# Local attention on 64x64 quarters of the matmul array: all of its products, and the last rows of the gated products

## The chip, the core and the metric

The kernel runs on one core of one Trainium2 chip. The metric is device time in microseconds (us): 3955.65 us is the median of three runs before the change (3954.25 to 3959.32). The core has a matmul engine (PE in the profile, with its weight loads as PEld), VectorE (DVE), ScalarE (ACT), GpSimd (POOL), and DMA queues, of which SyncE's (SP) carries nearly all of the traffic here. Matmuls write to PSUM, eight banks of 128 partitions x 512 fp32 values; VectorE and ScalarE carry the results on to SBUF.

## The reference, cut to what matters

A block of eight sequences of 512 tokens and 256 channels goes through three residual steps: a small transformer (two layers, added with the factor 0.5), a global attention, and the small transformer once more. All is fp32. One layer of the small transformer, as far as it matters here:

```python
def _layer(x, wqkv, qs, ksc, wo, lg, lb, w1, b1, w2, b2):
    h = shift_token(x)                        # second half of the channels from the token before
    q, k, v = jnp.split(h @ wqkv, 3, axis=-1) # 8 heads of 64
    q, k = rotary_xpos(l2norm(q) * qs, l2norm(k) * ksc)
    x = x + local_attention(q, k, v) @ wo
    h = layernorm(shift_token(x)) * lg + lb
    a, g = jnp.split(h @ w1 + b1, 2, axis=-1) # 682 and 682 channels
    return x + (a * gelu(g)) @ w2 + b2
```

In `local_attention` a window has 128 tokens; queries of a window see their own window and the one before:

```python
    sim = jnp.einsum('bhwid,bhwjd->bhwij', bq, bk)
    mask = (i < j) | (i > j + WINDOW) | (j == -1)
    attn = jax.nn.softmax(jnp.where(mask, -big, sim), axis=-1)
    out = jnp.einsum('bhwij,bhwjd->bhwid', attn, bv)
```

So query i of a window sees the keys 0 to i of its own window and the keys i to 127 of the window before. In halves of 64: the second half of the own keys is seen by the second half of the queries only, and the first half of the keys of the window before by the first half of the queries only.

## The kernel before

A sequence is 4 tiles of 128 tokens, and a window is one tile. Two streams, `stream(0, ...)` and `stream(1, ...)`, each take four sequences through the small transformer twice, eight blocks a stream, and a third stream (`global_stream`) computes the global attention, head by head, of sequences whose first transformer is done. The three are Python generators that only record operations.

The order in which operations are issued is not written down. `Plan.record` collects each operation with its inputs and outputs, and `Plan.order` schedules them greedily: at each step it takes, on the engine that can start earliest, the operation of lowest rank that is ready within 40 ns. It uses the costs of `Plan.cost`, keeps a pool of slots for every buffer (the eight PSUM banks among them), and for the matmul engine it counts a change of array shape: an operation's shape is its `op.mode`, a change is priced by `MODE`, and `STICK` lets operations of the present shape go first. Operations recorded within `plan.together()` stay together. `Plan.issue` then issues every operation from one line, L369, so the profile tells groups apart by the names of their tiles.

The array can be used whole (128 rows x 128 columns of weights), in two halves by rows (64x128: `halves`), by columns (128x64: `columns`), in four quarters (64x64: `quarters`), or in strips of 32 rows (`fours`, used for the scores of the global attention). Products on different parts run side by side.

`attention(k, y, l, far)` handles one sequence and layer. `front(t)` makes q, k and v of tile t; `scores(t, ...)` the probabilities; `values(t, ...)` the products with v; `project(t, o)` the output projection. `far` is true for blocks 1 to 6 of a stream (24 attentions) and false for the first and the last block (8 attentions, called "near" in this text). The two forms differ in how they turn tiles: far turns q, k and the probabilities with VectorE's 32x32 transposes and a round trip through DRAM; near uses transposes on the matmul engine, which go to a PSUM bank and are copied by ScalarE (`work_both` in the profile).

Before the change:

- Scores of far tiles 1 to 3 (`quarters` in the code) run in four 64x64 quarters and leave out the masked half windows (192 of 256 columns). Scores of near tiles and of far tile 0 run in two halves, one head of a pair in each, with 128 query columns of weights and 128 or 256 key columns moving. The two heads of a pair go to two banks.
- Values of far tiles 1 to 3 run in quarters, the two halves of the keys into two PSUM banks, `pos[0]` and `pos[1]`. ScalarE copies the first to `o`, and VectorE adds the second. Values of near tiles and of far tile 0 run by columns, all 128 keys of a window at once, one bank `po`, which ScalarE copies to `o`.
- In `glu`, the hidden width is 682 = 5 x 128 + 42. The last 42 rows and one row for the bias (43 in all) of two token tiles lie at partitions 0 and 64; their products run in two halves, one per tile, at the end of each pair of tiles.

Of the kernel before, what the change touches and what calls it, by code (L numbers as in the profile page):

```python
# [15 lines left out]
P = 128  # L16
B, N, D = 8, 512, 256
NT = N // P
DEPTH, HEADS, DH, WINDOW = 2, 8, 64, 128
INNER = HEADS * DH  # L20
NPAIR = HEADS // 2
HID = int(D * 4 * 2 / 3)
NHC = -(-HID // P)
FULL = NHC - 1
LAST = HID - FULL * P
HALF = P // 2
# [150 lines left out]
class Plan:  # L177
# [55 lines left out]
    def cost(self, op):  # L233

        if op.engine == "tensor":

            lanes, op.mode = {}, "whole"
            for name, args, kw in op.calls:
                lane, t = 0, 109.0
                if name == "matmul":  # L240
                    a = kw["lhsT"]
                    lane, t = (a.region()[0], args[0].region()[0]), 2 * max(0.842 * elements(kw["rhs"]), 0.852 * a.shape[1])
                    k, m = a.shape
                    op.mode = "fours" if k <= 32 else "quarters" if k == m == 64 else "halves" if k <= 64 else "columns" if m <= 64 else "whole"
                lanes[lane] = lanes.get(lane, 0.0) + t
            busy = max(lanes.values())
            return busy, busy + 170
        name, args, kw = op.calls[0]
        n = max(elements(a) for a in (*args, *kw.values()) if hasattr(a, "shape"))
        if name == "dma_start":  # L250
            return 580.0, 2300.0
        if op.engine == "scalar":
            if name == "activation":
                op.mode = {AF.Exp: "exp", AF.Gelu: "gelu"}.get(args[2])
                busy = 70 + 0.82 * n + (105 if "bias" in kw else 0)
                return (busy + 93, busy + 310) if "accum_out" in kw else (busy, busy + 110)
            return 70 + 0.81 * n, 175 + 0.81 * n
        if op.engine == "vector":
            if name == "tensor_tensor_reduce":
                return 90.0 + n, 250.0 + n  # L260
            if name == "bn_stats":
                return 70.0 + n, 150.0 + n
            return 90 + 1.035 * n, 170 + 1.035 * n
        if name == "memset":
            return 80 + 0.85 * n, 100 + 0.85 * n
        if ALU.pow in args:
            return 350.0 + 157 * n, 400.0 + 157 * n
        return 210 + 1.98 * n, 250 + 1.98 * n
# [107 lines left out]
def macaron(ctx: ExitStack, tc: tile.TileContext, x, weight, wqkv, wo, w1, w2, b2, vecs, qk_scales, rotary, out):  # L376
    nc = plan = Plan()
# [121 lines left out]
    def bank(shape):  # L499
        return psum.tile(shape, F32, tag="bank", width=N)  # L500
# [65 lines left out]
    def attention(k, y, l, far):  # L566
# [5 lines left out]
        v = {}  # L572
# [57 lines left out]
        def scores(t, pair, rn):  # L630
# [14 lines left out]
            nk = min(t, 1) + 1  # L645
            kinds = slice((t + 1) % 2, (t + 1) % 2 + nk)
            mk = mask[:, kinds, :].rearrange("p j k -> p (j k)")
            probs = []
# [3 lines left out]
            for g in range(2):  # L652

                quarters = far and nk == 2
                sps = [bank([P, 2, 3 * HALF if quarters else nk * P]) for _ in range(2)]

                pieces = [(slice(0, P), slice(0, nk * P), slice(0, nk * P))]
                if quarters:

                    pieces = []  # L660
                    for half in range(2):
                        q = slice(half * HALF, (half + 1) * HALF)
# [6 lines left out]
                with plan.together():  # L669
                    for i in range(2):  # L670
                        keys = kT[:, 2 * g + i].rearrange("p j k -> p (j k)")
                        for q, to, ks in sorted(pieces, key=lambda piece: piece[1].start - piece[1].stop):
                            for par in range(2):
                                rows = slice(par * DH, (par + 1) * DH)
# [17 lines left out]
                for par in range(2):  # L692
                    for i in range(2):
                        h = 2 * i + par
# [11 lines left out]
                for par in range(2):  # L706
                    for i in range(2):
                        h = 2 * i + par
# [23 lines left out]
        def values(t, probs):  # L732

            nk = min(t, 1) + 1
            o = work.tile([P, NPAIR, P], F32, tag="o", bufs=2)
            if far and nk == 2:

                pos = [bank([P, NPAIR, P]) for _ in range(2)]
                for g in range(2):
                    with plan.together():  # L740
                        for i in range(2):
                            for n in range(2):
                                for half in range(2):

                                    j = (1 - half, half)[n]
                                    q = slice(half * 2, half * 2 + 2) if n else slice(0, 4)
                                    rows = slice(half * HALF, (half + 1) * HALF)
                                    for par in range(2):
                                        h = 2 * i + par
                                        hd = 4 * g + h  # L750
                                        nc.tensor.matmul(
                                            pos[half][par * DH : (par + 1) * DH, 2 * g + i, q.start * 32 : q.stop * 32],
                                            lhsT=v[t - 1 + j][rows, hd * DH : (hd + 1) * DH],
                                            rhs=probs[g][rows, j, q, h, :],
                                            start=(n == 0),
                                            stop=(n == 1),
                                        )
                nc.scalar.copy(o, pos[0])
                nc.vector.tensor_add(o, pos[1], o)
                return o  # L760
            po = bank([P, NPAIR, P])

            def products(pair, turned):
                for j in range(nk):
                    for par in range(2):
                        hd = 2 * pair + par
                        nc.tensor.matmul(
                            po[par * DH : (par + 1) * DH, pair, :],
                            lhsT=v[t - (t + j) % 2][:, hd * DH : (hd + 1) * DH],
                            rhs=turned(par, j),  # L770
                            start=(j == 0),
                            stop=(j == nk - 1),
                        )

            if far:
                for g in range(2):
                    with plan.together():
                        for i in range(2):
                            products(2 * g + i, lambda par, j: probs[g][:, j, :, 2 * i + par, :])
            else:  # L780
                turned = []
                for n in range(NPAIR + 2):
                    if n < NPAIR:
                        pt = bank([P, 2, nk, P])
                        for par in range(2):
                            for j in range(nk):
                                nc.tensor.transpose(pt[:, par, j, :], probs[n // 2][:, n % 2 * 2 + par, j * P : (j + 1) * P], ident)
                        pT = work.tile([P, 2, nk, P], F32, tag="both", bufs=2, width=2 * N)
                        nc.scalar.copy(pT, pt)
                        turned.append(pT)  # L790
                    if n >= 2:
                        with plan.together():
                            products(n - 2, lambda par, j: turned[n - 2][:, par, j, :])
            nc.scalar.copy(o, po)
            return o

        def project(t, oT):
# [9 lines left out]
        for t in range(NT):  # L807
            probs = scores(t, *qn)
# [6 lines left out]
            o = values(t, probs)  # L815
# [3 lines left out]
    def glu(k, y, step, xb, far):  # L819
        l = step % DEPTH  # L820
        w1_sb, ends_sb, w2_sb = glu_weights[step]

        if far:
            sh = work.tile([P, NT, P], F32, tag=f"qn{k}", bufs=2)
            tokens = later(k)
            for tiles in (slice(0, NT - 1), slice(NT - 1, NT)):
                rows = tokens[1 + tiles.start * P : 1 + tiles.stop * P, :]
# [26 lines left out]
        for c in range(2):  # L854
            h = zpool.tile([P, N + 1], F32, tag=f"z{k}", bufs=2)
# [8 lines left out]
        us = []  # L864
        for m in range(FULL):
            if m < 4:
                if m % 2 == 0:
                    pair = work.tile([P, 2, N], F32, tag=f"p{k}", bufs=2)
# [21 lines left out]
        with plan.together():  # L890
            for turn in range(2):
                half = slice(turn * N // 2, (turn + 1) * N // 2)
                for c in range(2):
                    nc.tensor.matmul(
                        ag[: TAIL + LAST, turn],
                        lhsT=ends_sb[:, c, TAIL * turn : TAIL * turn + TAIL + LAST],
                        rhs=hT[c][:, half],
# [12 lines left out]
        pys = {}  # L910
        for t in (0, 2, 1, 3):
            py = bank([P, D])
            pys[t] = py
            with plan.together():
                for m in range(FULL):
                    nc.tensor.matmul(py, lhsT=us[m][:, t * P : (t + 1) * P], rhs=w2_sb[:, m, :], start=(m == 0), stop=False)
            if t < 2:
                continue
            with plan.together():
                for at, q in ((0, t - 2), (TAIL, t)):  # L920
                    rows = slice(at, at + LAST + 1)
                    nc.tensor.matmul(
                        pys[q],
                        lhsT=us[FULL][rows, q * P : (q + 1) * P],
                        rhs=w2_sb[rows, FULL, :],
                        start=False,
                        stop=True,
                    )
            for q in (t - 2, t):
                nc.vector.tensor_add(y[:, q, :], pys[q], y[:, q, :])  # L930
                if l == DEPTH - 1:
                    nc.vector.scalar_tensor_tensor(xb[:, q, :], y[:, q, :], 0.5, xb[:, q, :], ALU.mult, ALU.add)
            yield
# [215 lines left out]
```

## Time and profile before

| what | value |
|---|---|
| the profiled execution's own time | 3959.6 us |
| its span, first to last instruction | 3957.8 us |
| granted clock of the matmul engine, mean | 0.995 |
| VectorE adds into `work_o` | 72, 49.1 us busy |
| ScalarE copies into `work_o` | 128, 74.7 us busy |
| values by columns, near: 128x64, 128 columns | 896 rows, 66.1 us busy |
| values by columns, far tile 0: 128x64, 128 columns | 384 rows, 30.0 us busy |
| scores in halves: 64x128, 256 columns | 384 rows, 50.8 us busy |
| scores in halves: 64x128, 128 columns | 512 rows, 37.5 us busy |
| last rows of the gated products: 43x128, 256 columns | 256 rows, 37.4 us busy |
| quarters, all products | 7680 rows |

How to read it: a group of the profile names engine, operation, output and inputs, then (for matmuls) rows x columns of weights and the shape that moves, and the number of rows in the trace. An fp32 product has two rows of its own, a transpose one. Busy time of a group is the time in which at least one of its instructions ran. In a timeline, a line stands for neighbouring rows of one group: start, length, group, number of rows, and in brackets the idle time before it with the engine that ended it.

### The profile page before, as it was taken

How to read it: one execution, taken by the hardware profiler on the slowest of the kernel's cores; microseconds unless marked ns; L12 is line 12 of the kernel's file. 1: busy time of each engine (PE TensorE's matmuls, PEld its weight loads, DVE VectorE, ACT ScalarE, POOL GpSimd, SP SyncE). 2: the span in 40 equal slices, each digit the busy share in tenths (PEclk: the TensorE clock that was granted, in tenths of full speed). 3: DMA queues.
4: the chain of work that ended last, by engine and by line, in shares of the span. 5: the costliest groups of instructions: out<-in, count | busy, mean ns of one | idle time of the engine just before them, and what ended most of it. 6: DMA issues, size and time to landing. Idle time of an engine off the chain costs nothing.

```text
span 3957.8 us, 67863 instructions
## 1 busy us (share of the span) xinstructions
PE 3892.5 (98%) x23808; PEld 2675.0 (68%) x23808; DVE 2422.4 (61%) x6832; ACT 1779.5 (45%) x4556; POOL 1226.6 (31%) x1132
## 2 busy tenths in 40 slices
PE   8999999999999999999999999999999999999998
PEld 5565776766767667676676766767677666677665
DVE  7575655666566665665765667566556665526573
ACT  5564434535344353453544545354345353324462
POOL 6242323434133241331523424143223231103240
PEclk9999999999999999999999999999999999999999
DMA  3000543534435244352443534435325344110000
GB/s 116 1 23 28 153 137 103 154 98 138 124 119 148 87 142 119 118 153 86 138 142 101 156 93 143 137 102 161 96 90 154 93 132 128 57 37 5 1 23 11
DMA packets 437625, 400.43 MB, mean 101 GB/s; under 512 B 53954, under 2 KB 379172, under 8 KB 437284
## 3 DMA queue, kind: packets, MB, share of 16 engines
q1 hardware_dynamic: 436420, 394.76, 33.7%
q8 instruction: 189, 3.10, 0.3%
q10 hardware_dynamic: 864, 1.33, 0.1%
q14 instruction: 152, 1.25, 0.1%
HBM read 235.49 MB, written 143.66 MB: 96 GB/s over the span
## 4 chain that ended last, share of the span: by engine, by line
PE 55%; DVE 3%; ACT 2%; issue 2%; POOL 1%; DMA 0%; SPq 0%; POOLq 0%; DVEq 0%; ACTq 0%
PE psum_bank L369 55%; ACT work_p L369 1%; DVE work_p L369 1%; DVE work_qn L369 1%; POOL small_rn L369 0%; DVE small_ss L369 0%; POOL work_t L369 0%; SPq L369 0%; ACT work_qn L369 0%; DVE xpool_x L369 0%; DMA work_both<-dram_turned 0%; DMA work_p<-dram_turned 0%; ACT work_sq L369 0%; DVE work_both L369 0%; ACT work_both L369 0%
## 5 line engine op out<-in xcount | busy, mean ns | idle before, releaser
L369 PE MATMUL psum_bank<-work_xw,work_e 128*128 128x256 f32 x4096 | 959.5, 384 | 3.6 <-ACT work_e L369 2.5
L369 PEld LDWEIGHTS psum_bank<-work_xw,work_e 128*128 128x128 f32 x4096 | 762.6, 190 | 203.4 <-issue 42.3
L369 PE MATMUL psum_bank<-wpool_wqkv,zpool_z 128*128 128x512 f32 x1536 | 703.6, 597 | 1.3 <-ACT work_o L369 1.3
L369 ACT ACTIVATE work_p<-work_p,small_nmax,small_rn 128x192 f32<-128x192 f32 (+2 forms) x1024 | 543.8, 533 | 288.9 <-DVE small_nmax L369 187.0
L369 POOL TENSOR_TENSOR work_t<-work_qn,const_tab 128x256 f32<-128x256 f32 x512 | 388.7, 780 | 713.3 <-ACT work_qn L369 691.7
L369 PE MATMUL psum_bank<-zpool_z,wpool_w 128*128 128x512 f32 x1280 | 560.9, 597 | 1.5 <-DVE zpool_z L369 1.2
L369 POOL TENSOR_TENSOR work_p<-work_p,small_ri 128x768 f32<-128x768 f32 (+1 forms) x192 | 267.6, 1395 | 871.2 <-DVE small_ri L369 410.0
L369 POOL TENSOR_TENSOR small_rn<-small_ss,const_nhalf 128x8 f32<-128x8 f32 x256 | 486.7, 1902 | 137.8 <-DVE small_ss L369 130.9
L369 PE MATMUL psum_bank<-work_wa,work_gz 128*128 128x256 f32 x2048 | 477.4, 381 | 3.0 <-DVE work_gz L369 2.8
L369 ACT ACTIVATE work_e<-psum_bank 128x512 f32<-128x512 f32 x512 | 298.7, 596 | 396.6 <-PE psum_bank L369 390.1
L369 PEld LDWEIGHTS psum_bank<-wpool_wqkv,zpool_z 128*128 128x128 f32 x1536 | 284.4, 191 | 276.6 <-issue 261.6
L369 PEld LDWEIGHTS psum_bank<-zpool_z,wpool_w 128*128 128x128 f32 x1280 | 244.2, 192 | 302.2 <-issue 279.8
L369 PEld LDWEIGHTS psum_bank<-work_wa,work_gz 128*128 128x128 f32 x2048 | 384.9, 190 | 73.2 <-issue 14.9
L369 DVE SCALAR_TENSOR_TENSOR xpool_x<-psum_bank,gsmall_rinv,xpool_x 128x256 f32<-128x256 f32 x512 | 242.9, 476 | 275.0 <-PE psum_bank L369 272.2
L369 ACT COPY work_qn<-psum_bank 128x512 f32<-128x512 f32 x256 | 148.5, 583 | 374.8 <-PE psum_bank L369 322.9
L369 DVE TENSOR_REDUCE small_ss<-work_sq 128x8 f32<-128x512 f32 x256 | 172.5, 674 | 133.7 <-ACT work_sq L369 133.1
L369 DVE SCALAR_TENSOR_TENSOR work_p<-psum_bank,const_vec,work_p 128x512 f32<-128x512 f32 x128 | 95.8, 749 | 252.6 <-PE psum_bank L369 203.4
L369 PE MATMUL psum_bank<-wpool_wo,work_o 128*128 128x256 f32 x1024 | 246.7, 384 | 2.5 <-DVE work_o L369 1.6
L369 DVE COPY work_xw<-psum_bank 128x512 f32<-128x512 f32 x256 | 174.2, 681 | 121.8 <-PE psum_bank L369 120.5
L369 PE MATMUL psum_bank<-wpool_w,work_p 128*128 128x256 f32 x1024 | 242.7, 380 | 0.0
L369 DVE TENSOR_TENSOR ypool_y<-psum_bank,ypool_y 128x256 f32<-128x256 f32 x256 | 101.7, 419 | 216.2 <-PE psum_bank L369 213.2
L369 ACT COPY work_o<-psum_bank 128x512 f32<-128x512 f32 x128 | 74.7, 583 | 340.8 <-PE psum_bank L369 335.7
(89 smaller groups left out, 5025.8 us busy)
## 6 DMA issues: line engine op xcount, KB each, us to landing
work_p<-dram_quarters SPq DMA_DIRECT2D x576, 128.0 KB
dram_quarters<-work_p SPq DMA_DIRECT2D x288, 192.0 KB
dram_turned<-work_both SPq DMA_DIRECT2D x96, 512.0 KB
work_both<-dram_turned SPq DMA_DIRECT2D x384, 128.0 KB
work_wa<-in_weight_dram SPq DMA_DIRECT2D x128, 256.0 KB
wpool_w<-in_w_dram SPq DMA_DIRECT2D x48, 640.0 KB
work_hT<-work_gz SPq DMA_DIRECT2D x512, 32.0 KB
dram_turned<-work_p SPq DMA_DIRECT2D x48, 256.0 KB
```

Of the source, the lines that this page charges most:

```text
L369: getattr(getattr(nc, op.engine), name)(*map(real, args), **{k: real(a) for k, a in kw.items()})
```

## The change

Every product named above in halves or by columns is moved to quarters, and the planner's test for `quarters` is widened to fit 43-row products.

- Scores outside the far case are cut in two by queries: twice as many products, each with 64 query columns of weights and the same key columns.
- `values` has one form for all tiles: keys in halves of 64 rows, two banks, as far tiles 1 to 3 had it. With two windows, each pair of heads has four products of 128 query columns and four of 64; for tile 0 two of each. ScalarE copies `pos[0]` to `o`, VectorE adds `pos[1]`, for tile 0 only the second half of the queries.
- The last rows of the gated products are cut in two by tokens.

The number of products rises from 12480 to 13696, and that of VectorE adds into `work_o` from 72 to 128.

```diff
@@ Plan.cost @@
-                    op.mode = "fours" if k <= 32 else "quarters" if k == m == 64 else "halves" if k <= 64 else "columns" if m <= 64 else "whole"
+                    op.mode = "fours" if k <= 32 else "quarters" if k <= 64 and m <= 64 else "halves" if k <= 64 else "columns" if m <= 64 else "whole"
@@ attention, scores @@
-                pieces = [(slice(0, P), slice(0, nk * P), slice(0, nk * P))]
+                pieces = [(slice(q, q + HALF), slice(0, nk * P), slice(0, nk * P)) for q in (0, HALF)]
@@ attention, values @@
-            if far and nk == 2:
-
-                pos = [bank([P, NPAIR, P]) for _ in range(2)]
...
-                nc.scalar.copy(o, pos[0])
-                nc.vector.tensor_add(o, pos[1], o)
-                return o
-            po = bank([P, NPAIR, P])
-
-            def products(pair, turned):
-                for j in range(nk):
-                    for par in range(2):
-                        hd = 2 * pair + par
-                        nc.tensor.matmul(
-                            po[par * DH : (par + 1) * DH, pair, :],
-                            lhsT=v[t - (t + j) % 2][:, hd * DH : (hd + 1) * DH],
-                            rhs=turned(par, j),
-                            start=(j == 0),
-                            stop=(j == nk - 1),
-                        )
+
+            pos = [bank([P, NPAIR, P]) for _ in range(2)]
+
+            def products(pair, moving):
+
+                for n in range(2):
+                    for half in range(2):
+                        own = half == n
+                        if nk == 1 and not own:
+                            continue
+                        rows = slice(half * HALF, (half + 1) * HALF)
+                        q = slice(half * HALF, (half + 1) * HALF) if n else slice(0, P)
+                        for par in range(2):
+                            hd = 2 * pair + par
+                            nc.tensor.matmul(
+                                pos[half][par * DH : (par + 1) * DH, pair, q],
+                                lhsT=v[t if own else t - 1][rows, hd * DH : (hd + 1) * DH],
+                                rhs=moving(par, own, rows, q),
+                                start=(n == 0 or nk == 1),
+                                stop=(n == 1 or nk == 1),
+                            )
...
-                            products(n - 2, lambda par, j: turned[n - 2][:, par, j, :])
-            nc.scalar.copy(o, po)
+
+                            products(n - 2, lambda par, own, rows, q: turned[n - 2][rows, par, t % 2 if own else 1 - t % 2, q])
+            nc.scalar.copy(o, pos[0])
+            q = slice(HALF if nk == 1 else 0, P)
+            nc.vector.tensor_add(o[:, :, q], pos[1][:, :, q], o[:, :, q])
             return o
@@ glu, last rows @@
-                    nc.tensor.matmul(
-                        pys[q],
-                        lhsT=us[FULL][rows, q * P : (q + 1) * P],
-                        rhs=w2_sb[rows, FULL, :],
-                        start=False,
-                        stop=True,
-                    )
+                    for half in (0, HALF):
+                        nc.tensor.matmul(
+                            pys[q][half : half + HALF, :],
+                            lhsT=us[FULL][rows, q * P + half : q * P + half + HALF],
+                            rhs=w2_sb[rows, FULL, :],
+                            start=False,
+                            stop=True,
+                        )
```

More of the change, by code (lines that the diff above doesn't have):

```diff
@@ L735, in values @@
             o = work.tile([P, NPAIR, P], F32, tag="o", bufs=2)
-            if far and nk == 2:
-                pos = [bank([P, NPAIR, P]) for _ in range(2)]
[L739 to L747, printed above, removed]
-                                    for par in range(2):
-                                        h = 2 * i + par
-                                        hd = 4 * g + h
-                                        nc.tensor.matmul(
[L752 to L756, printed above, removed]
-                                        )
-                nc.scalar.copy(o, pos[0])
-                nc.vector.tensor_add(o, pos[1], o)
-                return o
@@ L761, in values @@
-            po = bank([P, NPAIR, P])
-            def products(pair, turned):
-                for j in range(nk):
-                    for par in range(2):
-                        hd = 2 * pair + par
-                        nc.tensor.matmul(
-                            po[par * DH : (par + 1) * DH, pair, :],
-                            lhsT=v[t - (t + j) % 2][:, hd * DH : (hd + 1) * DH],
-                            rhs=turned(par, j),
-                            start=(j == 0),
-                            stop=(j == nk - 1),
-                        )
+            pos = [bank([P, NPAIR, P]) for _ in range(2)]
@@ L778, in values @@
                         for i in range(2):
-                            products(2 * g + i, lambda par, j: probs[g][:, j, :, 2 * i + par, :])
+                            products(
+                                2 * g + i,
+                                lambda par, own, rows, q: probs[g][rows, own * (nk - 1), q.start // 32 : q.stop // 32, 2 * i + par, :],
+                            )
             else:
@@ L921, in glu @@
                     rows = slice(at, at + LAST + 1)
-                    nc.tensor.matmul(
-                        pys[q],
-                        lhsT=us[FULL][rows, q * P : (q + 1) * P],
-                        rhs=w2_sb[rows, FULL, :],
-                        start=False,
-                        stop=True,
-                    )
+                    for half in (0, HALF):
[5 more added lines that the diff above has]
+                            stop=True,
+                        )
             for q in (t - 2, t):
```

## The prediction

> **What bounds the kernel now.** I read the page's busy times first, then its slices, then the waits of TensorE, then the stretches by stage, then the timeline of TensorE alone.
>
> ```profile
> PE 3892.5 (98%) x23808; PEld 2675.0 (68%) x23808; DVE 2422.4 (61%) x6832; ACT 1779.5 (45%) x4556; POOL 1226.6 (31%) x1132
> ...
> PEclk9999999999999999999999999999999999999999
> ```
>
> TensorE is busy 98% at the full granted clock, VectorE 61%. A busy PE is not a PE at its peak, so I looked at how its time is built up.
>
> ```profile
> 0.00:430.00 430.00, 400.74 (x2119) 259.15 (x2120) 285.03 (x847) 234.08 (x558) 157.27 (x166) 0.99 0.16 49
> 430.00:3600.00 3170.00, 3157.49 (x19913) 2198.26 (x19913) 1919.80 (x5361) 1370.44 (x3579) 969.05 (x873) 1.00 0.40 118
> 3600.00:3957.00 357.00, 334.27 (x1779) 217.57 (x1777) 217.59 (x625) 175.02 (x421) 100.25 (x94) 0.98 0.03 10
> ```
>
> The columns are length, then busy PE, PEld, DVE, ACT, POOL. In the middle (mostly "far" attention, filled up with the global heads) PE is idle 12.5 us of 3170. In the first 430 and the last 357 us, where the "near" form of the attention runs, it is idle 29 and 23 us. Those two ends are where another engine can set the pace.
>
> ```profile
> 413.56 1.89 PE L369 MATMUL psum_bank<-wpool_w,work_p 128*128 128x256 f32 x8
> 415.29 0.59 PE L369 MATMUL psum_bank<-wpool_w,work_qn 128*128 128x256 f32 x2
> 415.72 3.62 PE L369 MATMUL psum_bank<-work_xw,work_e 128*128 128x256 f32 x16
> 419.27 1.09 PE L369 MATMUL psum_bank<-work_p,work_v 128*64 128x128 f32 x16
> 420.29 0.70 PE L369 MATMUL psum_bank<-wpool_w,work_qn 43*128 43x256 f32 x4
> 420.93 1.53 PE L369 MATMUL psum_bank<-work_kT,work_qT 64*64 64x192 f32 x32
> 422.39 1.99 PE L369 MATMUL psum_bank<-wpool_wo,work_o 128*128 128x256 f32 x8
> 424.22 1.03 PE L369 MATMUL psum_bank<-work_xw,work_e 128*128 128x256 f32 x4
> ```
>
> These starts price everything. Each product has two rows (two passes). Within one array shape nothing is lost: 8 rows of 256 columns from 413.56 to 415.29 are 216 ns each. The rows' start times in the trace give 109 ns for 128 columns, 162.5 for 192 and 56 for 64, and rows on different parts of the array run side by side. At a change of shape time is lost: the 16 rows of 128x64 (two side by side, 8 x 0.109 = 0.87) take 1.02 us until the next shape starts; the four 43-row ones (2 x 0.216 = 0.43) take 0.64; the 32 quarters (four side by side, 8 x 0.1625 = 1.30) take 1.46. So a change costs about 0.15 us into shapes with 64 weight columns and about 0.20 into shapes with 128. Over all 922 changes of the trace I took medians: the first row starts 0.09 later than the columns before it explain, and its second pass is 0.05 late (64 columns) or 0.10 late (128).
>
> Adding up every product and change in this way gives 3848 us; TensorE's stream lasts from 13.0 to 3951.6, so 90 us are real waits, 59 of them in the two ends.
>
> **The change, part by part.**
>
> *Near values, tiles 1 to 3.* 8 near attentions x 3 tiles x 4 pairs = 96 pair products. Before, each lane (a half of the columns) has two products of 128 columns: 4 passes x 109 = 437 ns. After, each of four lanes has one of 128 and one of 64 columns: 2 x 109 + 2 x 56 = 330 ns. 96 x 107 ns = **-10.3 us**, all of it in the two ends. Tile 0 (8 near, 24 far) keeps 2 x 109 ns a pair: its longer lane stays 128 columns.
>
> *Scores of near tiles and of far tile 0, last rows of the gated products.* Twice the instructions, half the weight columns, four lanes instead of two, the same columns per lane: **0** in steady state. Waves of 64x256 and 43x256 in four lanes are not in the trace; the nearest row is 64*64 with 192 columns, which fits four lanes to 1%. So I take 0. Were they to run two at a time, 192 and 128 products would cost 41 + 28 us more; the row leaves no sign of that.
>
> Here a rule speaks against the change: the Trainium skill ("TensorE: Matmul & The Clock Gate", section "Wait — 56ns, not 53.3ns?") says that starts never come closer than about 25 ns. A wave of four would then last at least 100 ns, the 64-column passes would save 9 ns instead of 53, and the 10.3 us would shrink to 1.7. The trace disagrees:
>
> ```profile
> 503.83 0.90 PE L369 MATMUL psum_bank<-work_p,work_v 64*64 64x128 f32 x32
> 504.55 1.48 PE L369 MATMUL psum_bank<-work_kT,work_qT 64*64 64x192 f32 x32
> ```
>
> 32 rows, half of 128 and half of 64 columns, take 0.72 us with the entry: 22.5 ns each, and inside a wave the starts are 7 ns apart. I go by the row.
>
> *Changes of shape.* The order in which the two built programs issue their products (it holds no times) has 923 stretches of one shape before (388 whole, 206 quarters, 127 of 16 rows, 108 of 128x64, 94 of 64x128) and 851 after (382 whole, 343 quarters, 126 of 16 rows). Weighted with the medians (into quarters 0.14, into whole 0.19 to 0.20, or 0.15 where transposes come first, into 16 rows 0.19, into 64x128 0.20, into 128x64 0.14) the changes cost 158.4 before and 142.6 after: **-15.8 us**. A quarters stretch carries some 21 ns of staggered starts, the two old shapes 7 to 8: 137 x 21 - 202 x 7.5 ns = **+1.4**.
>
> TensorE's own work thus falls by 24.7 us: 15.1 in the two ends, 9.4 in the middle and 0.2 of rounding.
>
> *The added VectorE pass.* All tiles now end in ScalarE's copy plus a VectorE add from the second bank.
>
> ```profile
> L369 ACT COPY work_o<-psum_bank x128: 562/586/625, 53.3 to 3909.5; 128x512 f32<-128x512 f32 x128
> ...
> L369 DVE TENSOR_TENSOR work_o<-psum_bank,work_o x72: 646/688/693, 451.0 to 3375.5; 128x512 f32<-128x512 f32 x72
> ```
>
> 24 adds are full size (0.69 us) and 32 cover half the columns (0.42, from the 128x256 add into y): 16.5 + 13.4 = 30 us of VectorE, 20 of them in the ends, where it is busy 285 of 430 and 218 of 357 us. The add waits for ScalarE's copy; behind it on VectorE stand the score maxima and the scaling of the probabilities of the other stream, for which TensorE's transposes wait. For the output projection the new chain is 0.59 + 0.69 + signals, about 1.5 us. In the order of the new program, with the pass times above, TensorE has other work for less than that between values and projection at 3 of 128 places (0.2, 0.8 and 1.1 us); the sum of what lacks is 2.4 us (before: 0.5, against the 0.75 that ScalarE's copy alone needs). So **+2 us** on the path by this edge. The 24 half-size adds of far tile 0 hide: the middle has at least 1.7 us of products between the two. Without that cover they would cost 24 x 0.5 = 12 us.
>
> *The second bank.* The Trainium skill ("TensorEngine Tiling (Array Packing)", "Gotcha 1: PSUM Pressure") says that row tiles may not share a bank, hence the pair of banks (no run here tries one). In the order of the new program a bank is filled again within 1.5 us of its last product at 42 places in the two ends, before at 6. ScalarE's copy needs 0.59 and signals, two maxima about 0.9, the add 1.5. So many of these fit if the engine is free, and some don't. No row shows the cost: from -2 us to 42 x 0.35 = 15. I take it together with the next point.
>
> *What TensorE's saved time in the ends is worth.* Waits there come from chains through VectorE and ScalarE:
>
> ```profile
> PE psum_bank L369 <- DVE ypool_y L369: 16.7, 4, 13.0
> PE psum_bank L369 <- DVE work_p L369: 13.3, 16, 3.2
> PE psum_bank L369 <- DVE work_qn L369: 7.5, 8, 1.8
> PE psum_bank L369 <- ACT work_both L369: 4.4, 7, 1.1
> ```
>
> A faster TensorE reaches such waits earlier, and the chain is no shorter. I let half of the 15.1 us (7.5) turn into waits, the bank waits included; with the 2 us of the projection edge the ends keep 5.6. The middle keeps its 9.4, since PE has 99.6% there. Sum: 24.7 - 7.5 - 2 = **15.2 us**. The profiled execution itself took 3959.6 (span 3957.8); it becomes 3944.4. It stands 0.1% above the median of the runs shown, 3955.65, which becomes **3940.5**.
>
> **Rivals.** (1) The likeliest, as above, 3934 to 3947: chance 0.42. (2) *All of it is kept.* The ends are 93% PE after all, and fewer shapes give the planner freer choice: 3955.65 - 24.7 = 3931. For it: the waits are few and long, at layer ends, apart from where the products changed. Against: the tighter banks. Chance 0.28. (3) *The ends keep nothing*: waits on banks and on VectorE take the place of the 15.1 us and the projection edge stays: 3955.65 - 9.4 + 2 = 3948, on the border of no change: chance 0.22. (4) *Slower: VectorE becomes the bound of the two ends.* The ends gain nothing and the 20 us of adds there lie on its path, -9.4 + 20 = +10.6: 3966. It decides once VectorE's gaps lie in the wrong places: it has 145 + 139 us of idle time in the two ends against the 20 us added, but the attention parts within them are denser than the rest. Chance 0.08. That the change doesn't do what it says is excluded for the number of stretches, which the order shows; four lanes run two at a time would be +69 us, below 0.02 and counted with (4).
>
> The whole order of work shifts with the planner's new costs, and the 30-odd us of waits in the middle may fall otherwise: some 8 us either way, which blurs all four.
>
> **Numbers.** A measurement of this kernel can tell about 0.2% (8 us) from no change. Below 3947.7 lie (1), (2): 0.70; within, most of (3): 0.22; above 3963.6, (4): 0.08. The range leaves out (4) and the far end of (2): 3928 to 3957.
>
> **What would show it.** Right: five shapes become three, with about 850 changes; the 64*64 rows with 256 columns at 216 ns per wave of four; 128 work_o adds; the middle shorter by 9 us. Likeliest against (2): waits of PE for work_p, work_both and work_o in the first 430 and last 350 us grow by some 10 us. (4) would show as VectorE over 80% busy in the ends with PE waiting for work_o or small_peak. I would be wrong if the four-lane waves of 256 columns took over 216 ns, or if the waits in the middle changed by more than the 9 us.

## The result, and the profile after

The changed kernel takes 3946.97 us (median of 14 runs, 3942.57 to 3952.63) against 3955.66 beside it (14 runs). The ratio is 0.9975 with a 95% interval of 0.9968 to 0.9982: a gain of 8.7 us, small, with an interval clear of 1. The profiled execution took 3952.0 us, 5.0 more than the median; its span is 3950.1 (before: 3957.8).

The page's busy times, and then the windows of the two ends and the middle (busy PE, PEld, DVE, ACT, POOL):

```profile
PE 3878.5 (98%) x26240; PEld 2659.5 (67%) x26240; DVE 2447.9 (62%) x6888; ACT 1766.9 (45%) x4548; POOL 1233.7 (31%) x1132
```

```profile
0.00:430.00 430.00, 398.82 (x2893) 252.67 (x2894) 297.83 (x863) 246.54 (x568) 158.47 (x167) 0.99 0.16 50
430.00:3600.00 3170.00, 3155.21 (x20920) 2200.61 (x20919) 1928.50 (x5394) 1323.98 (x3547) 975.99 (x872) 1.00 0.40 119
3600.00:3950.00 350.00, 324.48 (x2431) 206.24 (x2429) 221.60 (x633) 196.41 (x433) 99.26 (x94) 0.97 0.03 10
```

TensorE does 2432 rows more in 14 us less of busy time; VectorE has 56 instructions and 25.5 us more. PE is idle 31, 15 and 26 us, a little more than before in every stretch. The timeline of TensorE at a place like the one shown in the prediction:

```profile
412.75 1.89 PE L369 MATMUL psum_bank<-wpool_w,work_p 128*128 128x256 f32 x8
414.48 0.59 PE L369 MATMUL psum_bank<-wpool_w,work_qn 128*128 128x256 f32 x2
414.91 3.62 PE L369 MATMUL psum_bank<-work_xw,work_e 128*128 128x256 f32 x16
418.45 0.98 PE L369 MATMUL psum_bank<-work_p,work_v 64*64 64x128 f32 x30
419.17 0.43 PE L369 MATMUL psum_bank<-wpool_w,work_qn 43*64 43x256 f32 x2
419.27 0.28 PE L369 MATMUL psum_bank<-work_p,work_v 64*64 64x128 f32 x2
419.38 0.60 PE L369 MATMUL psum_bank<-wpool_w,work_qn 43*64 43x256 f32 x6
419.66 1.62 PE L369 MATMUL psum_bank<-work_kT,work_qT 64*64 64x192 f32 x32
421.21 1.99 PE L369 MATMUL psum_bank<-wpool_wo,work_o 128*128 128x256 f32 x8
```

Values, last rows and scores follow each other in one shape: from 418.45 to 421.21 they take 2.76 us, where the three shapes of before took 3.12 (419.27 to 422.39). The 43*64 rows even start among the last values. This is what the change was said to do, and at such a place it does it. What TensorE waited for, with total, count and longest:

```profile
PE psum_bank L369 <- DVE ypool_y L369: 15.9, 4, 12.3
PE psum_bank L369 <- ACT work_both L369: 9.3, 16, 1.4
PE psum_bank L369 <- DVE work_o L369: 6.2, 9, 1.4
PE psum_bank L369 <- DVE work_p L369: 5.7, 10, 3.1
PE psum_bank L369 <- DVE work_qn L369: 5.4, 6, 1.1
PE psum_bank L369 <- DVE small_peak L369: 4.0, 7, 1.2
```

Waits for `work_both` (4.4 us before) and for VectorE's `work_o` (1.6 before) more than doubled, `small_peak` (the maxima, which free the banks of the scores) went from 1.5 to 4.0, and `work_p` more than halved from 13.3.

To find where 24.7 us of passes and changes went, I cut each trace by the rows of 192 columns (far tiles 1 to 3): the middle runs from the first to the last of them, the ends are the rest. "Sum" is passes and changes priced as in the prediction for that kernel's own order; "waits" is length minus sum; "half clock" is the part of them that the trace's clock records can explain at most: half the time in which the clock was granted at 0.5. All in us. Each row but for its median is of one execution, from 3.0 us under its kernel's median (e6) to 5.0 over it (changed).

| kernel | time, median | middle: length | sum | waits | half clock | ends: length | sum | waits | half clock |
|---|---|---|---|---|---|---|---|---|---|
| before | 3955.7 | 2903.1 | 2880.3 | 22.7 | 5.1 | 1035.5 | 967.8 | 67.7 | 13.7 |
| changed | 3947.0 | 2902.6 | 2870.0 | 32.6 | 8.5 | 1029.1 | 953.4 | 75.6 | 13.7 |
| e1 scores and last rows only | 3952.7 | 2906.0 | 2869.4 | 36.6 | 5.1 | 1026.8 | 968.8 | 58.0 | 6.8 |
| e2 values only | 3990.1 | 2906.5 | 2873.5 | 33.0 | 6.8 | 1066.2 | 962.3 | 103.9 | 25.6 |
| e3 near values by columns | 3950.8 | 2908.8 | 2870.0 | 38.8 | 13.7 | 1026.5 | 966.9 | 59.6 | 8.5 |
| e4 small add | 3958.6 | 2900.4 | 2870.0 | 30.3 | 5.1 | 1038.6 | 952.7 | 85.9 | 17.1 |
| e5 two banks, columns | 3976.4 | 2910.5 | 2878.9 | 31.6 | 6.8 | 1046.7 | 960.1 | 86.7 | 17.1 |
| e6 quarters, regrouped | 3963.1 | 2900.1 | 2870.0 | 30.1 | 5.1 | 1040.0 | 941.0 | 99.0 | 15.4 |
| e7 columns, regrouped | 3971.6 | 2902.6 | 2870.7 | 31.9 | 5.1 | 1050.2 | 954.3 | 95.9 | 18.8 |
| e8 changed, delay 120 | 3959.1 | 2903.3 | 2868.2 | 35.1 | 8.5 | 1034.3 | 958.1 | 76.1 | 13.7 |
| e9 before, seven banks | 3958.8 | 2901.9 | 2876.6 | 25.4 | 1.7 | 1035.3 | 967.4 | 67.9 | 10.2 |
| e10 before, delay 100 | 3963.8 | 2908.9 | 2878.0 | 30.9 | 6.8 | 1037.4 | 969.4 | 67.9 | 11.9 |
| e11 before, delay 120 | 3983.8 | 2928.0 | 2873.6 | 54.4 | 17.1 | 1036.9 | 973.0 | 63.9 | 8.5 |
| e12 changed, delay 100 | 3945.6 | 2896.0 | 2869.9 | 26.2 | 6.8 | 1027.6 | 951.3 | 76.3 | 10.2 |

The change cut the sum by 10.3 in the middle and 14.4 in the ends, and waits took back 9.9 and 7.9. Up to 3.4 us of the 9.9 are half clock, and none of the 7.9.

### The profile page after: what moved, and what is told of

Read it like the earlier page. It is cut to its first block, busy times and chain, and to the rows that moved or that the text cites. A ratio compares the mean times of both kernels' runs of the same rounds, so it can differ in the third digit from the quotient of the medians.

```text
span 3950.1 us, 72878 instructions
## 1 busy us (share of the span) xinstructions
PE 3878.5 (98%) x26240; PEld 2659.5 (67%) x26240; DVE 2447.9 (62%) x6888; ACT 1766.9 (45%) x4548; POOL 1233.7 (31%) x1132
## 4 chain that ended last, share of the span: by engine, by line
PE 81%; DVE 5%; issue 2%; ACT 2%; POOL 1%; DMA 0%; SPq 0%; DVEq 0%; POOLq 0%; ACTq 0%
PE psum_bank L369 81%; ACT work_p L369 2%; DVE work_p L369 2%; DVE work_qn L369 1%; DVE small_ss L369 1%; POOL small_rn L369 0%; POOL work_t L369 0%; ACT work_both L369 0%; DVE work_xw L369 0%; DVE small_bnst L369 0%; SPq L369 0%; DVE work_both L369 0%; DVE work_o L369 0%; DVE xpool_x L369 0%; POOL small_rstd L369 0%
## 5 line engine op out<-in xcount | busy, mean ns | idle before, releaser
L369 PE MATMUL psum_bank<-wpool_wqkv,zpool_z 128*128 128x512 f32 x1536 | 712.2, 603 | 2.7 <-ACT work_v L369 2.0
L369 POOL TENSOR_TENSOR work_t<-work_qn,const_tab 128x256 f32<-128x256 f32 x512 | 397.4, 797 | 590.3 <-ACT work_qn L369 503.5
L369 PEld LDWEIGHTS psum_bank<-wpool_wo,work_o 128*128 128x128 f32 x1024 | 191.4, 190 | 56.7 <-DVE work_o L369 16.1
L369 ACT ACTIVATE work_p<-psum_bank,const_vec 128x512 f32<-128x512 f32 x128 | 87.9, 687 | 296.6 <-PE psum_bank L369 288.0
```

The costliest lines, as they stand in the source:

```text
L369: getattr(getattr(nc, op.engine), name)(*map(real, args), **{k: real(a) for k, a in kw.items()})
```

## Experiments: which part makes the waits?

Theory N: the near values make them, by a second bank and VectorE's add. Theory F: whatever part saves TensorE time in the ends, chains through other engines turn it into waits. Theory O: the planner's new order decides, by chance. The kernels before ran beside them, and are what each ratio refers to, at 3957.0 (e1 to e4), 3957.6 (e5 to e8) and 3957.3 (e9 to e12).

**e1**: scores and last rows from the changed kernel, `values` from the one before.

> Only the scores and the last rows of the gated products run in quarters; all values stay as before (by columns and one bank for near tiles and far tile 0). Passes and changes of shape in its order sum to 3838 us (before 3848, changed kernel 3823). Theory N (the waits that came with the change are made by the near values: two banks and an add): its waits stay those of before, 108, so 3946, level with the changed kernel. Theory F (any time that TensorE saves where it waits for chains turns into waits, whatever part saves it): this part saves only 1.6 us in the two ends, so also about 3946. Theory O (the planner's new order decides by chance): anywhere within 8 us of 3948.

Measured: 3952.74, ratio 0.9993 (0.9985 to 1.0002), within O's range and over the 3946 of N and F. The ends have no added waits (58.0, before 67.7), as N says. The middle saved 10.9 of sum and got 13.9 more waits, which neither N nor F had placed there.

**e2**: the kernel before, with `values` alone from the changed one.

> Only the values run in quarters with two banks and the add; scores and last rows stay in halves. Passes and changes sum to 3836 us. Theory N: the waits are those of the changed kernel, 124, so 3960, slower than before by 4. Theory F: about 5 us are saved in the ends and half of that stays, the middle keeps 7: 3955.7 - 7 - 2.5 = 3946.

Measured: 3990.11, ratio 1.0083 (1.0069 to 1.0097), far over both. The sign is N's, the size nobody's: the ends wait 103.9, and why so long stays open.

**e3**: the changed kernel, near tiles with the old products.

```diff
         def values(t, probs):
+            return quartered(t, probs) if far else columned(t, probs)
...
```

> The changed kernel, but the near values by columns in one bank with ScalarE's copy alone, as before; far tile 0 stays in quarters. The middle has the changed kernel's changes of shape (647), passes and changes sum to 3837 us, 13.5 more than the changed kernel, all of that in the two ends. Theory N: the near values' saving is eaten by the waits that they make, so 3944 to 3948, no slower than the changed kernel. The forecast's own weights (half of the saving in the ends kept, 2 us for the add): 3947 + 4.5 = 3951. Theory F gives 3951 too.

Measured: 3950.80, ratio 0.9982 (0.9975 to 0.9988), overlapping the changed kernel's interval. The number is F's and the forecast's, 3 us over N's; the waits lie where N has them. In the ends they are 59.6; with the near values in quarters they are 75.6. So that part, alone, saves 13.5 of sum and pays 16.0 in waits, up to 5.2 of them half clock: the ends of the two traces are 1026.5 without it and 1029.1 with it. TensorE's waits in e3 show the old picture:

```profile
PE psum_bank L369 <- DVE ypool_y L369: 15.6, 3, 12.3
PE psum_bank L369 <- DVE work_p L369: 13.5, 16, 3.3
PE psum_bank L369 <- DVE work_qn L369: 7.8, 9, 1.8
PE psum_bank L369 <- ACT work_both L369: 4.7, 8, 1.1
```

`work_p` is back at 13.5 and `work_both` at 4.7, as before the change. N holds as far as it names the part; in it, three suspects remained: the add, the bank, the slots of `work_both`.

**e4**: the add cut to one query column of 128 in near tiles; the rest of the second half of the sum is left out.

```diff
             q = slice(HALF if nk == 1 else 0, P)
+            if not far:
+                q = slice(P - 1, P)
             nc.vector.tensor_add(o[:, :, q], pos[1][:, :, q], o[:, :, q])
```

> The changed kernel, but in near tiles VectorE adds only the last of 128 query columns of each pair from the second bank (the rest of the second half of the sum is left out): the bank is held nearly as long, the add costs some 0.1 us in place of 0.69 or 0.42. Passes and changes sum to 3823 us, as in the changed kernel. If the add (its time on VectorE and in the chain to the output projection) makes the added waits of the ends: 3947 - 10 to 16 = 3931 to 3937. If the banks or the earlier arrival of TensorE make them: 3944 to 3947.

Measured: 3958.63, ratio 1.0005 (0.9996 to 1.0013), over both expectations, and slower than the changed kernel with less work. Waits of the ends: 85.9. A shorter add does not take the waits away. But the planner knows its cost and ordered the ends anew, so what the add costs in the changed kernel's own order is not shown.

**e5**: near values by columns, but in two banks, one per head of a pair (edit against e3).

```diff
-            nc.scalar.copy(o, po)
+            nc.scalar.copy(o[:DH], pos[0][:DH])
+            nc.vector.tensor_copy(o[DH:], pos[1][DH:])
```

> Near values by columns as in e3, but the two heads of a pair go to two banks, held as long as the changed kernel holds its two; ScalarE copies one half of the partitions, VectorE the other (0.69 us, no wait of one for the other). Nothing is in quarters that was not in e3. Passes and changes sum to 3839 us (e3 3837, measured 3951, its waits in the two ends 59). If holding the second bank makes the added waits of the ends: 59 becomes 75 or more, 3965 to 3975. If not: 3951 to 3956.

Measured: 3976.42, ratio 1.0043 (1.0030 to 1.0057), just over the range for the bank; ends 86.7. Without a single near value in quarters the waits are there, with the same mark as in the changed kernel, `work_both`:

```profile
PE psum_bank L369 <- DVE ypool_y L369: 19.0, 7, 12.7
PE psum_bank L369 <- ACT work_both L369: 14.3, 15, 2.3
PE psum_bank L369 <- DVE work_p L369: 6.5, 10, 3.2
```

So F is not needed: e5 saves TensorE nothing against e3 (3839 us of passes and changes against 3837; the ends' sum is 6.8 smaller because 50 rows more fall into the middle), and the waits of the ends rise by 27, up to 8.6 of them half clock. Two banks emptied by two engines are enough, in this order.

**e6 and e7**: the turned probabilities of all four pairs first (in eight slots in place of two), then all products of the tile together, in quarters (e6) and by columns (e7).

```diff
-                        pT = work.tile([P, 2, nk, P], F32, tag="both", bufs=2, width=2 * N)
+                        pT = work.tile([P, 2, nk, P], F32, tag="e", bufs=2 * NT, width=N)
...
+                for g in range(0, NPAIR, 4):
+                    with plan.together():
+                        for n in range(g, g + 4):
+                            products(n, ...)
```

> The changed kernel, but the four turned pieces of the probabilities of a near tile go to the eight idle slots of the global attention's buffer (two shared slots before), and the products of all four pairs follow together. The two banks are open only for that stretch, and TensorE has 37 changes of shape fewer in the near parts: passes and changes sum to 3811 us (changed kernel 3823). If the waits of the ends come from the long hold of the two banks or from the two slots, they fall back to 60: 3811 + 108 = 3919. If they come from VectorE's add or from TensorE's early arrival: 3811 + 124 = 3935. If the planner's order decides by chance: 3927 plus or minus 12.

> The same regrouping with the near values by columns, one bank and ScalarE's copy alone (as in e3). Passes and changes sum to 3825 us. With waits as in e3 (114): 3939. If the near values in quarters are a gain once nothing holds them up, e6 is faster than this by up to their 14 us; if the add and the second bank cost as much as TensorE saves whatever the grouping, the two are within 4 us.

Measured: 3963.11 (ratio 1.0016, 1.0010 to 1.0023) and 3971.61 (1.0032, 1.0019 to 1.0044), both far over every expectation. The sums fell as priced (941.0 in the ends of e6), the waits rose to 99.0 and 95.9. In e6 TensorE now waits for the scaled probabilities:

```profile
PE psum_bank L369 <- DVE work_p L369: 30.3, 25, 5.4
PE psum_bank L369 <- DVE ypool_y L369: 19.5, 8, 12.1
```

13.3 us before, 30.3 here. My reading, which no run shows: the products that filled TensorE's time until the next probabilities came are issued later, all at once. Between the two forms, quarters are 8.5 us faster, of the 13.3 that their ends' sum is less. So the quarters can pay here; this grouping costs more than they bring. With the two banks open only for one short stretch, quarters have 3.1 us more waits in the ends than columns, in place of 16.0: a hint that the length of the hold matters.

**e9**: the kernel before with seven banks in place of eight.

> The kernel before with seven PSUM banks in place of eight; the same work, passes and changes sum to 3844 us (before 3848). If banks limit the two ends, its waits there rise from 70 to 80 or more, as with the changed kernel's second bank, and the time to 3963 or more; if the ends have banks to spare, waits stay at 70 and the time is 3951 to 3957.

Measured: 3958.84, ratio 1.0005 (0.9996 to 1.0014), 2 us over the range for banks to spare; ends 67.9 as with eight. In its built order (traces show no bank numbers) a bank of the ends is filled again within 1.5 us of its last product at 35 places (before 7, where the prediction has 6; changed 42, e5 37, e4 52, e2 59). So tight banks alone, which I had made the cause, do not make the waits. What the held pair needs besides (both banks free at once, or VectorE as second engine at the end of every near tile) is not told apart by these runs; a version in which ScalarE alone empties both banks was not tried.

**e8, e10, e11, e12**: one constant of the planner moved, the assumed delay of a signal; the work is the same.

```diff
-    SIGNAL = 110.0
+    SIGNAL = 120.0
```

(100 in e10 and e12; before in e10 and e11, changed in e8 and e12.)

> The changed kernel with one constant of the planner moved (the assumed signal delay 110 to 120 ns): the same work in another order; passes and changes sum to 3826 us. How far chance in the order goes: if it is small beside the 16 us of added waits in the ends, 3946 to 3953 and 70 to 80 us of waits there; if it is large, anything from 3935 to 3965.

> The kernel before with the planner's assumed signal delay at 100 in place of 110 ns; passes and changes sum to 3847.5 us. How far order alone goes: 3948 to 3964; if it goes less far than the change did, within 4 us of 3956.

> The kernel before with the assumed signal delay at 120 ns; passes and changes sum to 3846.6 us. As for 100 ns: 3948 to 3964, or within 4 us of 3956 if order matters less than the change.

> The changed kernel with the assumed signal delay at 100 ns; passes and changes sum to 3821 us (changed kernel 3823; with 120 ns 3826, measured 3959). If the change is worth its 9 us whatever the order, 3944 to 3949; if the order decides, anywhere from 3940 to 3962.

Measured: changed 3959.12 (1.0004, 0.9996 to 1.0012) with 120 and 3945.59 (0.9968, 0.9956 to 0.9981) with 100; before 3963.84 (1.0018, 1.0009 to 1.0026) with 100 and 3983.78 (1.0066, 1.0053 to 1.0078) with 120, 20 us over what I had allowed for order. Order alone moves the kernel before by 28 us and the changed one by 13, more than the change did. In the kernel before it acts in the middle: 22.7, 30.9 and 54.4 us of waits in three orders, while the ends stay at 64 to 68. In the changed kernel the ends wait 76 us in all three orders, and it acts on the sum of the ends too (951.3 to 958.1). Theory O holds for the middle; in the ends N names the part that adds the waits, and its reason (bank and add) is not shown. The kernel before stands in the best of its three orders. The means over three orders are 3967.8 before and 3950.6 after, 17 us apart; three orders a side make that a hint and no more. No run beat the changed kernel beyond the intervals; e12 is level with it.

## Why the prediction held, point by point

The forecast was 15.2 us less, 3940.5, in a range of 3928 to 3957; measured are 8.7 less. The range held with some luck: in another order of the same work (e8) the changed kernel takes 3959.1.

- *What bounds it.* Right. Passes and changes of shape explain 98% of TensorE's stream before and 97% after, with prices taken from the trace of before.
- *Near values, -10.3, and doubled products, 0.* Right. A wave of four with 256 columns lasts 216 ns at 64 rows and 216 to 220 at 43 (median from the row starts), and one of four with 64 columns 56 ns: 14 ns a start, under the 25 ns that the prediction quotes.
- *Changes, -15.8.* Right by count (850) and by price: the medians of the new trace are 144 ns into quarters and 194 into whole, as before.
- *The add's own chain, +2.* About right. TensorE's waits for `work_o` are 3.5 us before (VectorE's and ScalarE's) and 6.9 after. The last one of the kernel is the place with 0.2 us of cover in the prediction's count:

```profile
3899.18 1.05 PE L369 MATMUL psum_bank<-work_both,work_v 64*64 64x128 f32 x32 [0.29 <-ACT work_both L369]
3901.63 1.99 PE L369 MATMUL psum_bank<-wpool_wo,work_o 128*128 128x256 f32 x8 [1.40 <-DVE work_o L369]
```

- *The ends keep 5.6.* They became 6.4 us shorter: 14.4 less of sum, 7.9 more of waits, where I had 15.1 and 9.5. The size was right by luck, the reason was not: I let any time saved by TensorE turn half into waits, but the near values alone bring 16.0 us of waits (changed against e3), and the other parts take 8.1 away (e3 against before). "The second bank", which I had folded into that half, was nearer the cause, though e9 shows that a missing bank is not enough.
- *"The middle keeps its 9.4, since PE has 99.6% there."* This step failed. The sum fell by 10.3 and the waits rose by 9.9, so the middle kept 0.5. A stage in which TensorE is busy 99.6% can still get new waits from a new order, and the order before was the best of three (e10, e11). A third of the 9.9, up to 3.4 us, is the clock. The forecast had named 8 us of chance either way for the middle; that shortfall decided between 3940.5 and 3947.
- *Its own signs.* Three came: 850 changes, 216 ns a wave, 128 adds. "The middle shorter by 9 us" did not (0.5), and a sign of being wrong did: the waits in the middle changed by more than 9 us (9.9). The waits for `work_p`, `work_both` and `work_o` that were to grow by some 10 us in the ends hardly grew (18.4 us before, 19.1 after): `work_p` fell as the other two rose.

The rivals: "all is kept" fell with the waits of the ends, "VectorE becomes the bound" with VectorE at 298 of 430 and 222 of 350 us, 69% and 63%. The time fell next to the rival in which the ends keep nothing, and for another reason: the middle kept nothing.

## What to carry to other kernels

Price a change of array shape by the starts of neighbouring rows, and take the count from the built order; here that arithmetic explains 97 to 98% of the stream, and the rest is waits. Where a scheduler orders the work, move one of its constants slightly on both sides before you believe a gain of a few tenths of a per cent: the order alone did three times that. A saving that asks for a second bank and a second engine to empty it should be tried alone: here it saved 13.5 us and brought 16.0 of waits, and the medians with it and without it (3947.0 and 3950.8) cannot be told apart.

## What the runs showed of the hardware

The clock of the matmul engine can fall to half where the profile counts TensorE as busy almost throughout. The timeline and the windows of the changed kernel (clock in the column after POOL) around 2037 us:

```profile
2034.00 2.50 PE L369 MATMUL psum_bank<-work_hT 16*128 16x512 f32 x8
2036.43 0.90 PE L369 MATMUL psum_bank<-work_p,work_v 64*64 64x128 f32 x32
2038.54 3.78 PE L369 MATMUL psum_bank<-work_xw,work_e 128*128 128x256 f32 x8 [1.22 <-ACT work_e L369]
2042.12 2.48 PE L369 MATMUL psum_bank<-wpool_wqkv,zpool_z 128*128 128x512 f32 x3
```

```profile
2032.00:2037.00 5.00, 5.00 (x128) 3.39 (x128) 2.00 (x10) 1.32 (x5) 0.00 (x0) 1.00 0.31 100
2037.00:2044.00 7.00, 5.78 (x27) 3.89 (x20) 2.39 (x5) 3.68 (x13) 1.47 (x1) 0.52 0.47 129
```

The granted clock is 0.52 for 7 us, and eight rows of 256 columns take 3.58 us, 447 ns each in place of 216. The clock records give such stretches in pieces of 3.4 us, 39.8 us of the span before and 45.6 after.

The wait of 1.22 us is hardly what brought it. The records have the half clock from 2037.35 to 2044.18, and by the profile's modelled ends the wait begins at 2037.33; in e3 the half clock begins at the same place 0.17 us ahead of the wait. The wait of 1.40 us at 3900, shown above, passes at full clock. What stands ahead is another thing: the eight rows of the global scores (`work_hT`, strips of 32 rows) take 2.43 us to the next group, in place of 1.07, the median of such stretches. All four half-clock stretches in the changed kernel's middle follow rows of this group that were drawn out so; yet e4, in the same order, passes two of the same places (1449 and 1732 us) at full clock. What sets the clock back stays open. The Trainium skill ("TensorE: Matmul & The Clock Gate", section "What's actually happening") has the half clock follow an idle window of about 3.4 us; no wait as long as that stands ahead of any of the four, and the measurement decides.

How much hangs on it shows by luck: the changed kernel, e3, e4 and e6 issue the same 9922 products in the same order throughout the middle. It lasts 2902.6, 2908.8, 2900.4 and 2900.1 us; without the half clock's 8.5, 13.7, 5.1 and 5.1 these are 2894.1, 2895.1, 2895.3 and 2895.0. The order fixed the waits to about 1 us, and the clock added 5 to 14. It shows between executions of one kernel too: of the changed kernel's 14, the fastest (3942.57 us) had a mean granted clock of 0.998 and the slowest (3952.63) 0.994.
